# Moving six of 400 gathers from GpSimd to SyncE, one row at a time

## The chip, the cores and the metric

The kernel runs on one core of one Trainium2 chip. The metric is the device time of one execution in microseconds (us), the median of several runs. The core has five engines with a queue of instructions each: TensorE (PE: matrix products and transposes, weight loads shown apart as PEld), VectorE (DVE), ScalarE (ACT), GpSimd (POOL) and SyncE (SP), which here only issues DMAs. All DMAs of the core run on the same 16 DMA engines.

## The reference

The inputs are `seq` (1024 x 50 item numbers), `lengths` (1024), a table `emb` of 100001 rows of 128 floats, whose row 0 counts as zeros, and `gamma` and `beta`, 128 each.

```python
e = emb[seq]                                   # 1024 x 50 x 128
prefix = jnp.cumsum(e, axis=1)
denom = jnp.minimum(t_idx[None, :], lengths[:, None])
uF = prefix / denom[:, :, None]
mean, var = uF.mean(axis=0), uF.var(axis=0)    # over the 1024 sequences
y = (uF - mean) * lax.rsqrt(var + BN_EPS) * gamma + beta
def step(v, x):                                # 50 steps in time
    v = v + (x - v) / TAU
    spike = (v - V_TH >= 0)
    return v - spike * V_TH, spike
uF_out = spikes.mean(axis=0)                   # 1024 x 128
scores = uF_out @ emb.T                        # 1024 x 100001
```

## The kernel before

The work has two stages. In the **first**, the 50 time steps run one after the other. A step t needs 1024 rows of the table, one for each sequence. They are fetched by eight indirect DMAs of GpSimd (line 207, `gather(t)`), each of which brings 128 rows of 512 bytes into a 128 x 128 block of the tile `e_t`: partition p of block n holds the row of sequence 8p + n. Two tiles `e` alternate (`gp`, two buffers), and `gather(t + 2)` stands in the program behind the transposes of step t, since it writes the tile that these have read. For each block TensorE transposes the rows and adds them into the running sum in PSUM (line 324, tiles `pre`, two halves of 512 sequences). VectorE scales the sum (line 335), takes its statistics (336, 342), and with ScalarE makes the normalized input, the state `v` and the spike counts (298, 301, 353, 359 to 372, 376, 379, 294). The order in which the instructions stand on each engine is the order of the program text; nothing reorders them afterwards.

In the **second** stage the counts, 128 features by 1024 sequences, are the weights of matrix products with the transposed table (`product`, line 160), and the results go out as `scores`, 409.6 MB (line 169, from SyncE). The counts are in three tiles: `countA` for the first 128 sequences, `countB` for the next 512, `countC` for the last 384. They are written at the end of step 49 and read to the end of the kernel. The table is loaded for this stage in pieces of 1024 rows (`fetch`, line 109). The first loads, some 20 MB, stand at the front of SyncE's queue; at t = 44 one more follows there (line 405), and then the stores of `scores`.

DMAs that SyncE and ScalarE issue report to eight counters in turn (DMAHW0 to DMAHW7), and a DMA is issued only once the one before it on its counter has landed: at most eight are under way. GpSimd's DMAs do the same with DMASW0 to DMASW7.

Of the kernel before, what the change touches and what calls it, by code (L numbers as in the profile page):

```python
# [12 lines left out]
F32 = mybir.dt.float32  # L13
BF16 = mybir.dt.bfloat16
F32R = mybir.dt.float32r
I32 = mybir.dt.int32
U32 = mybir.dt.uint32
AF = mybir.ActivationFunctionType
ALU = mybir.AluOpType

P = 128
# [4 lines left out]
BANK = 512  # L26
# [4 lines left out]
ASIDE = 2  # L31
SHIFT = TWICE + ASIDE
FURTHER = {5: 1, 6: 2}

WIDTHS = 4 * [2] + 4 * [3] + 13 * [6]
NARROW, MIDDLE = 4, 8
# [3 lines left out]
def rec_kernel(  # L40
# [9 lines left out]
    nc = tc.nc  # L50
    B, T = seq.shape
    N, D = table.shape
    NB = B // P
# [6 lines left out]
    const = ctx.enter_context(tc.tile_pool(name="const", bufs=1))  # L60
# [6 lines left out]


    countA = const.tile([P, P], F32R, tag="countA", name="countA")
    countB = const.tile([P, BANK], F32R, tag="countB", name="countB")  # L70
    countC = const.tile([P, B - BANK - P], F32R, tag="countC", name="countC")
    counts = [countA]
    counts += [countB[:, k : k + P] for k in range(0, BANK, P)]
    counts += [countC[:, k : k + P] for k in range(0, B - BANK - P, P)]
    ident = const.tile([P, P], F32, tag="ident", name="ident")


# [94 lines left out]
    with ExitStack() as ph:  # L172
# [6 lines left out]
        vp = ph.enter_context(tc.tile_pool(name="v", bufs=1, space=bass.MemoryType.PSUM))  # L179

        idx = once.tile([P, NB, T], I32, tag="idx", name="idx")
# [21 lines left out]

        def gather(t):
            es[t] = gp.tile([P, B], F32, tag="e", name=f"e_{t}")
            for n in range(NB):
                nc.gpsimd.indirect_dma_start(  # L207
                    out=es[t][:, n * P : (n + 1) * P],
                    out_offset=None,
                    in_=table,  # L210
                    in_offset=bass.IndirectOffsetOnAxis(ap=idx[:, n, t : t + 1].bitcast(U32), axis=0),
                )

        make_identity(nc, ident)
        isz = up.tile([P, NB, P], F32, tag="uF", name="isz")
        rb = up.tile([P, NB, P], F32, tag="uF", name="rb")
        gather(0)

        nc.vector.memset(isz, 0.0)
        for u in (0, P // 2):  # L220
# [70 lines left out]
        def over(t, v):  # L291

            d = lp.tile([P, B], BF16, tag="d", name=f"d_{t}")
            nc.scalar.activation(d, v, AF.Identity, bias=less)  # L294
            return d

        def rest(d, v, cs):
            nc.vector.scalar_tensor_tensor(negv[:, cs], d[:, cs], 0.0, v[:, cs], ALU.is_ge, ALU.subtract)
# [18 lines left out]
        for t in range(T):  # L317
            last = t == T - 1
            e = es.pop(t)
            uF = up.tile([P, B], F32, tag="uF", name=f"uF_{t}")  # L320
            bs = sp.tile([P, B // BANK, 6], F32, tag="bs", name=f"bs_{t}")
            for h, cs in enumerate(halves):
                for k in range(0, BANK, P):
                    nc.tensor.matmul(  # L324
                        pre[h][:, k : k + P],
                        lhsT=e[:, h * BANK + k : h * BANK + k + P],
                        rhs=ident,
                        start=False,
                        stop=last,
                        is_transpose=True,  # L330
                        skip_group_check=True,
                    )
                    if last and h and k + P < BANK:
                        keep_busy(ident, KQ // 2)
                nc.vector.scalar_tensor_tensor(uF[:, cs], rlen[:, cs], 1.0 / (t + 1), pre[h], ALU.max, ALU.mult)  # L335
                nc.vector.bn_stats(bs[:, h, :], uF[:, cs])
            if t + 2 < T:
                gather(t + 2)
            if not last:
                correct(t + 1, l)  # L340
            mv = sp.tile([P, 2], F32, tag="mv", name=f"mv_{t}")
            nc.vector.bn_aggr(mv, bs.rearrange("p h s -> p (h s)"))  # L342


            r = sp.tile([P, 1], F32, tag="r", name=f"r_{t}")
            nc.scalar.activation(r, mv[:, 1:2], AF.Sqrt, bias=eps)  # L346
            if last:
# [12 lines left out]
            q = sp.tile([P, 1], F32, tag="q", name=f"q_{t}")  # L360
            a = sp.tile([P, 1], F32, tag="a", name=f"a_{t}")
            if last:
                nc.vector.tensor_scalar(q, w, r, r, ALU.mult, ALU.mult)
                nc.vector.scalar_tensor_tensor(q, q, 3.0, r, ALU.subtract, ALU.mult)
                vA = once.tile([P, P], F32, tag="r0n", name="vA")
                nc.vector.scalar_tensor_tensor(vA, centred, q, near, ALU.mult, ALU.add)
                nc.vector.scalar_tensor_tensor(countA, vA, -2.0 * V_TH, count[:, pieceA], ALU.is_le, ALU.add)
                nc.vector.tensor_mul(a, q, hgb[:, 0:1])
            else:
                nc.vector.scalar_tensor_tensor(q, mv[:, 1:2], BN_EPS, r, ALU.add, ALU.mult)  # L370
                nc.vector.tensor_scalar(q, q, r, 3.0, ALU.mult, ALU.subtract)
                nc.vector.tensor_scalar(a, q, r, hgb[:, 0:1], ALU.mult, ALU.mult)  # L372


            def x(vt, cs):
                nc.scalar.activation(vt, uF[:, cs], AF.Identity, bias=hgb[:, 1:2], scale=a)  # L376

            def step(vt, cs):
                nc.vector.scalar_tensor_tensor(vt, negv[:, cs], -0.5, vt, ALU.mult, ALU.add)  # L379

            if not last:
                vt = vp.tile([P, B], F32, tag=f"v{(t + 1) % 2}", name=f"v_{t}")
                x(vt, whole)
                if t:
                    spiked(count, whole, v)
                step(vt, whole)
                v = vt
                if t == T - 2:
                    spiked(count, whole, v)
                    moved = once.tile([P, P], F32, tag="r0hi", name="moved")  # L390
                    nc.vector.tensor_scalar_add(moved, v[:, pieceA], beta2)
                    near = once.tile([P, P], F32, tag="r0", name="near")
                    nc.vector.scalar_tensor_tensor(near, v[:, pieceA], V_TH, moved, ALU.is_ge, ALU.subtract)
                d = over(t, v)
                if t + 2 < T:
                    l = only(t + 2)

                if t in (T - 8, T - 6):
                    q = (t - T + 8) // 2
                    pair(q)  # L400
                    prepare(q, vp.tile([P, HALF], F32, tag="v0", name=f"pt_{q}"))
                    if q == TWICE - 1:
                        for k in range(TWICE):
                            rows[GROUP + ASIDE + k] = first[:, k, :]
                        nc.sync.dma_start(
                            out=first[:, :TWICE, :],
                            in_=table[(GROUP + ASIDE) * HALF : (GROUP + SHIFT) * HALF, :].rearrange(
                                "(q p k) d -> p q (k d)", p=P, k=KQ
                            ),
                        )  # L410

        keep_busy(near, 2 * KQ)
        for cs in (pieceB, pieceC):
            nc.scalar.activation(uF[:, cs], uF[:, cs], AF.Identity, bias=mv[:, 0:1], scale=-1.0)

# [45 lines left out]
    for c, W in enumerate(WIDTHS):  # L464
# [21 lines left out]
        def ready():  # L486
            nonlocal to_split, third
            if to_split < q2 + FURTHER.get(c, 0) and free:
                prepare(to_split, psum.tile([P, HALF], F32, tag="ps", name=f"pt_{to_split}"))
# [13 lines left out]
        for n, q in blockwise:  # L503
            if n not in os:
                pool, tag, most = turns[blocks % len(turns)]
                blocks += 1
                os[n] = pool.tile([P, most * HALF], F32, tag=tag, name=f"o_{c}_{n}")
            o = os[n]
# [27 lines left out]
            if n in (1, 4) and c >= MIDDLE and to_fetch < parts:  # L536
                g, k = divmod(to_fetch - SHIFT, GROUP)
# [26 lines left out]
```

## Time and profile before

| | us |
|---|---|
| median of three runs | 1571.3 (1571.26 to 1571.34) |
| profiled execution, its own span | 1570.1 |
| GpSimd busy, 400 gathers among 406 instructions | 381.0 |
| TensorE matmul busy | 1130.3 |
| VectorE busy | 948.4 |
| ScalarE busy | 674.3 |

The span of the profiled execution goes from its first to its last instruction; the median of the runs stands 1.2 us above it. A row of the timeline gives start, duration, engine, line, operation, written and read tile, how many were merged, and in brackets how long the engine was idle before it and what ended that. "SPq" and "ACTq" mark DMAs that SyncE and ScalarE issue; their duration is that of issuing, not of the transfer. A row of the waits gives the time in total, the number of times and the longest. A row of the windows gives the busy time of each engine in a stretch, then the granted TensorE clock, the share of the DMA engines' time and the GB/s moved.

### The profile page before, as it was taken

The page shows a single profiled execution, that of the slowest core. Times are in us where ns is not written, and L with a number is a line of the kernel's source. Part 1 is how long each engine was busy: PE and PEld are TensorE (multiplying, and loading weights), DVE is VectorE, ACT ScalarE, POOL GpSimd, SP SyncE. Part 2 cuts the span into 40 slices and gives each one's busy share as a digit, 9 for nine tenths or more (in the row PEclk, how much of TensorE's full clock was granted, in tenths as well). Part 3 has the DMA queues.
Part 4 walks back from the last instruction along what each step waited for, and adds up shares of the span by engine and source line. Part 5 has one row for each costly group of instructions (what it writes and reads, how often), then busy time and mean ns, then how long its engine had stood idle before and what let it go on. Part 6 is the DMA issues. An engine that isn't in the chain of part 4 may idle for free.

```text
span 1570.1 us, 12251 instructions
## 1 busy us (share of the span) xinstructions
PE 1130.3 (72%) x4464; PEld 803.4 (51%) x4464; DVE 948.4 (60%) x1126; ACT 674.3 (43%) x698; POOL 381.0 (24%) x406
## 2 busy tenths in 40 slices
PE   4544444444445998899878888887888878888884
PEld 2211111111122776667766666665666656666663
DVE  5777777767778656666555555555555545555552
ACT  2333333333333545555444444444444444444442
POOL 7777777777776000000000000000000000000000
PEclk9999999999995999999999899999999999899997
DMA  9711111111121999999999999999999999999998
GB/s 347 265 52 52 53 52 53 52 53 54 52 79 49 374 413 404 423 416 404 426 428 430 428 427 415 423 423 430 405 421 426 412 432 409 429 430 420 423 388 364
DMA packets 51457, 488.12 MB, mean 311 GB/s; under 512 B 10095, under 2 KB 10352, under 8 KB 30276
## 3 DMA queue, kind: packets, MB, share of 16 engines
q1 hardware_dynamic: 30896, 430.86, 65.3%
q0 software_dynamic: 12800, 26.24, 5.7%
q10 hardware_dynamic: 7700, 30.23, 4.7%
q8 instruction: 35, 0.57, 0.1%
q14 instruction: 26, 0.21, 0.0%
HBM read 77.69 MB, written 409.60 MB: 310 GB/s over the span
## 4 chain that ended last, share of the span: by engine, by line
DMA 51%; POOL 18%; PE 14%; issue 8%; DVE 5%; ACT 3%; POOLq 0%; ACTq 0%; SPq 0%; DVEq 0%
DMA scores<-o 44%; POOL e L207 18%; PE po L160 13%; DMA e<-in_L_rec_emb_table,idx 7%; DVE o L519 3%; ACT o L521 3%; DVE pairs L153 1%; ACT pairs L152 1%; PE pt L136 0%; PE pre L324 0%; ACT hi L152 0%; DVE lo L153 0%; DMA idx<-in_r_seq 0%; ACTq L521 0%; POOLq L560 0%
## 5 line engine op out<-in xcount | busy, mean ns | idle before, releaser
L519 DVE TENSOR_SCALAR o<-po 128x1024 f32<-128x1024 f32 (+1 forms) x390 | 466.4, 1214 | 324.6 <-DMA scores<-o 178.7
L521 ACT ACTIVATE o<-po 128x1024 f32<-128x1024 f32 x392 | 393.4, 1026 | 496.8 <-DMA scores<-o 352.6
L207 POOL DMA_INDIRECT e<-in_L_rec_emb_table,idx x400 | 380.3, 951 | 123.9 <-issue 110.4
L324 PE MATMUL pre<-ident,e 128*128 128x128 f32 x400 | 180.1, 463 | 227.1 <-DMA e<-in_L_rec_emb_table,idx 226.2
L160 PE MATMUL po<-pairs,countB 128*128 128x512 f32 (+1 forms) x1120 | 290.7, 406 | 58.0 <-ACT o L521 58.0
L160 PE MATMUL po<-pairs,countC 128*128 128x512 f32 (+1 forms) x840 | 241.2, 435 | 56.6 <-ACT o L521 48.4
L160 PEld LDWEIGHTS po<-pairs,countB 128*128 128x128 f32 x1120 | 210.9, 193 | 117.9 <-ACT o L521 75.6
L324 PEld LDWEIGHTS pre<-ident,e 128*128 128x128 f32 x400 | 73.5, 184 | 337.1 <-DMA e<-in_L_rec_emb_table,idx 336.2
L160 PEld LDWEIGHTS po<-pairs,countC 128*128 128x128 f32 x840 | 169.0, 209 | 108.4 <-ACT o L521 60.1
L153 DVE TENSOR_TENSOR pairs<-pt,pairs 128x1024 fp32r<-128x1024 f32 x70 | 85.2, 1218 | 96.6 <-ACT pairs L152 96.5
L335 DVE SCALAR_TENSOR_TENSOR uF<-rlen,pre 128x512 f32<-128x512 f32 x100 | 68.3, 683 | 110.3 <-PE pre L324 110.3
L136 PE MATMUL pt<-ident,rows 128*128 128x128 f32 (+1 forms) x768 | 105.9, 284 | 9.7 <-issue 4.9
L346 ACT ACTIVATE r<-mv,eps 128x1 f32<-128x1 f32 x50 | 14.8, 295 | 222.5 <-DVE mv L342 222.5
L136 PEld LDWEIGHTS pt<-ident,rows 128*128 128x128 f32 (+1 forms) x768 | 95.4, 148 | 27.1 <-issue 11.4
L160 PE MATMUL po<-hi,countB 128*128 128x512 f32 x208 | 86.0, 413 | 12.0 <-ACT o L521 11.7
L282 PE MATMUL pre<-zT,ls 128*128 128x512 f32 x100 | 78.1, 783 | 22.8 <-DVE uF L335 18.9
L152 ACT CAST pairs<-pt 128x1024 fp32r<-128x1024 f32 x70 | 70.1, 1013 | 42.2 <-PE pt L136 42.2
L160 PE MATMUL po<-lo,countB 128*128 128x512 f32 x208 | 83.4, 401 | 0.0
L294 ACT ACTIVATE d<-v,less 128x1024 bf16<-128x1024 f32 x49 | 54.6, 1114 | 65.4 <-DVE v L379 62.3
L160 PE MATMUL po<-hi,countC 128*128 128x512 f32 x156 | 67.0, 429 | 15.7 <-ACT o L521 14.0
L376 ACT ACTIVATE v<-uF,hgb,a 128x1024 f32<-128x1024 f32 x49 | 59.2, 1208 | 30.5 <-DVE a L372 30.5
L160 PE MATMUL po<-pairs,countA 128*128 128x512 f32 x280 | 69.1, 396 | 4.2 <-ACT o L521 4.1
(88 smaller groups left out, 856.0 us busy)
## 6 DMA issues: line engine op xcount, KB each, us to landing
scores<-o SPq DMA_DIRECT2D x96, 3072.0 KB, 19.7
scores<-o SPq DMA_DIRECT2D x32, 1536.0 KB, 8.9
scores<-o SPq DMA_DIRECT2D x29, 1024.0 KB, 7.1
rows<-in_L_rec_emb_table ACTq DMA_DIRECT2D x19, 1536.0 KB, 29.7
scores<-o SPq DMA_DIRECT2D x8, 2896.5 KB, 17.1
rows<-in_L_rec_emb_table SPq DMA_DIRECT2D x5, 3072.0 KB, 34.6
e<-in_L_rec_emb_table,idx POOLq DMA_INDIRECT x400, 2.5
rows<-in_L_rec_emb_table SPq DMA_DIRECT2D x2, 1024.0 KB, 5.4
```

The source lines that it names most:

```text
L136: nc.tensor.transpose(pt[:, k0 : k0 + pw], r[:pw, k0 : k0 + D], ident[:pw, :pw])
L152: nc.scalar.copy(vh, vp)
L153: nc.vector.tensor_tensor(vl, vp, vh.bitcast(F32), ALU.subtract)
L160: nc.tensor.matmul(po[:, :kw], lhsT=counts[n], rhs=part[:, k0 : k0 + kw], start=j == 0, stop=j == 1,)
L207: nc.gpsimd.indirect_dma_start(out=es[t][:, n * P : (n + 1) * P], out_offset=None, in_=table, in_offset=bass.IndirectOffsetOnAxis(ap=idx[: ...
L282: nc.tensor.matmul(pre[h], lhsT=l, rhs=zT[:, h * BANK : (h + 1) * BANK], start=t == 0, stop=False, skip_group_check=True,)
L294: nc.scalar.activation(d, v, AF.Identity, bias=less)
L324: nc.tensor.matmul(pre[h][:, k : k + P], lhsT=e[:, h * BANK + k : h * BANK + k + P], rhs=ident, start=False, stop=last, is_transpose=True, ...
L335: nc.vector.scalar_tensor_tensor(uF[:, cs], rlen[:, cs], 1.0 / (t + 1), pre[h], ALU.max, ALU.mult)
L376: nc.scalar.activation(vt, uF[:, cs], AF.Identity, bias=hgb[:, 1:2], scale=a)
L519: nc.vector.tensor_scalar_mul(o[:, h0 : h0 + hw], po[:, :hw], 1.0 / T)
L521: nc.scalar.mul(o[:, h0 : h0 + hw], po[:, :hw], 1.0 / T)
```

## The change

In the steps 12, 19, 26, 33, 40 and 47 GpSimd fetches seven blocks instead of eight. The 128 rows of the eighth block are fetched by SyncE. To begin with, VectorE copies the item numbers of block 7 as floats, TensorE turns them (steps on the partitions, sequences along the row), and VectorE multiplies them by 512 and writes them as integers: the byte address of each row. SyncE loads sixteen addresses at a time into sixteen registers (line 226 of the new text, TENSOR_LOAD) and issues sixteen DMAs of 512 bytes with the registers as source addresses (line 229), eight times for one block. The six blocks go to four places in turn in the memory of `countB` (`held_rows`); the addresses stand in that of `countC` (`ids`). Both counts are now allocated behind the last step. `fetch_singles(0)` stands before the steps, and `fetch_singles(i + 1)` at the step that uses block i; on SyncE nothing stands between them.

```diff
+BY_SYNC = (12, 19, 26, 33, 40, 47)
+AT_ONCE = 16
...
+    held_rows = const.tile([P, BANK], F32, tag="countB", name="held_rows")
+    ids = const.tile([P, B - BANK - P], F32, tag="countC", name="ids")
...
         def gather(t):
-            for n in range(NB):
+            for n in range(NB - (t in BY_SYNC)):
                 nc.gpsimd.indirect_dma_start(
...
+        byte_rows = table.rearrange("n d -> (n d)").bitcast(U8)
+        starts = ids[:T, :P].bitcast(I32)
+        regs = [nc.sync.alloc_register(f"row{k}") for k in range(AT_ONCE)]
+        def fetch_singles(i):
+            t = BY_SYNC[i]
+            rows_of = held_rows[:, i % (BANK // P) * P :][:, :P]
+            singles[t] = rows_of
+            for p0 in range(0, P, AT_ONCE):
+                nc.sync.load(regs, starts[t : t + 1, p0 : p0 + AT_ONCE])
+                for k, reg in enumerate(regs):
+                    at = nc.sync.snap(reg, donate=True, min_val=0, max_val=(N - 1) * row_bytes)
+                    nc.sync.dma_start(
+                        out=rows_of[p0 + k : p0 + k + 1, :].bitcast(U8),
+                        in_=byte_rows[bass.ds(at, row_bytes)].rearrange("(o b) -> o b", o=1),
+                    )
...
         gather(0)
+        last_ids = ids[:, P : P + T]
+        nc.vector.tensor_copy(last_ids, idx[:, NB - 1, :])
+        ips = vp.tile([P, B], F32, tag="v0", name="ips")
+        nc.tensor.transpose(ips[:T, :P], last_ids, ident)
+        nc.vector.tensor_scalar_mul(starts, ips[:T, :P], float(row_bytes))
+        fetch_singles(0)
...
-                        lhsT=e[:, h * BANK + k : h * BANK + k + P],
+                        lhsT=singles[t] if h * BANK + k + P == B and t in singles else e[...],
...
                 gather(t + 2)
+            if t in BY_SYNC[:-1]:
+                fetch_singles(BY_SYNC.index(t) + 1)
```

On SyncE, at the end of the first loads of the table, this stood before (the name behind DMA is the written tile, then the read one; in brackets what it waits for). The load of line 405 follows directly:

```order
L109 DMA rows_112<-in_L_rec_emb_table 128x6x1024 [waits DMAHW2_49]
L109 DMA rows_114<-in_L_rec_emb_table 128x6x1024 [waits DMAHW3_49]
L109 DMA rows_116<-in_L_rec_emb_table 128x6x1024 [waits DMAHW4_49]
L405 DMA rows_103<-in_L_rec_emb_table 128x2x1024 [waits DMAHW5_49,DVE_49,PE_49]
L169 DMA scores<-o_0_2398 128x512 [waits DMAHW6_49,Activation_49]
```

And this stands there now (`held_rows` is the place of the single rows):

```order
L110 DMA rows_114<-in_L_rec_emb_table 128x6x1024 [waits DMAHW3_49]
L110 DMA rows_116<-in_L_rec_emb_table 128x6x1024 [waits DMAHW4_49]
L226 TENSOR_LOAD ids [waits DVE_49]
L229 DMA held_rows<-in_L_rec_emb_table 1x512 [waits DMAHW5_49]
L229 DMA held_rows<-in_L_rec_emb_table 1x512 [waits DMAHW6_49]
L229 DMA held_rows<-in_L_rec_emb_table 1x512 [waits DMAHW7_49]
L229 DMA held_rows<-in_L_rec_emb_table 1x512 [waits DMAHW0_49]
L229 DMA held_rows<-in_L_rec_emb_table 1x512 [waits DMAHW1_49]
L229 DMA held_rows<-in_L_rec_emb_table 1x512 [waits DMAHW2_49]
L229 DMA held_rows<-in_L_rec_emb_table 1x512 [waits DMAHW3_49]
L229 DMA held_rows<-in_L_rec_emb_table 1x512 [waits DMAHW4_49]
```

768 single rows and 48 register loads now stand between the last of the first loads and the load of line 405. The eighth single row uses the same counter, DMAHW4, as the last large load.

On TensorE, the end of step 12 (`e_641` is the tile of that step, `pre_182` the second half of the sum) before:

```order
L324 MATMUL pre_182<-ident,e_641 128x128 [waits DMASW4_49]
L324 MATMUL pre_182<-ident,e_641 128x128 [waits DMASW5_49]
L324 MATMUL pre_182<-ident,e_641 128x128 [waits DMASW6_49]
L324 MATMUL pre_182<-ident,e_641 128x128 [waits DMASW7_49]
L282 MATMUL pre_181<-zT,ls 128x512 [waits DVE_49]
```

And now (`e_781` is the tile of step 12):

```order
L351 MATMUL pre_322<-ident,e_781 128x128 [waits DMASW4_49]
L351 MATMUL pre_322<-ident,e_781 128x128 [waits DMASW5_49]
L351 MATMUL pre_322<-ident,e_781 128x128 [waits DMASW6_49]
L351 MATMUL pre_322<-ident,held_rows 128x128 [waits DMAHW4_49,DMAHW5_49,DMAHW3_49,DMAHW6_49,DMAHW2_49,DMAHW7_49,DMAHW1_49,DMAHW0_49]
L309 MATMUL pre_321<-zT,ls 128x512 [waits DVE_49]
```

The last of the eight transposes of the step waits for SyncE's counters in place of GpSimd's.

More of the change, by code (lines that the diff above doesn't have):

```diff
@@ L17 @@
 U32 = mybir.dt.uint32
+U8 = mybir.dt.uint8
 AF = mybir.ActivationFunctionType
@@ L69, in rec_kernel @@
     countA = const.tile([P, P], F32R, tag="countA", name="countA")
[L70 to L74, printed above, removed]
+    held_rows = const.tile([P, BANK], F32, tag="countB", name="held_rows")
+    ids = const.tile([P, B - BANK - P], F32, tag="countC", name="ids")
     ident = const.tile([P, P], F32, tag="ident", name="ident")
@@ L212, in gather @@
                 )
+        byte_rows = table.rearrange("n d -> (n d)").bitcast(U8)
+        row_bytes = 4 * D
+        starts = ids[:T, :P].bitcast(I32)
+        regs = [nc.sync.alloc_register(f"row{k}") for k in range(AT_ONCE)]
+        singles = {}
+        def fetch_singles(i):
[10 more added lines that the diff above has]
+                    )
         make_identity(nc, ident)
@@ L325, in rec_kernel @@
                         pre[h][:, k : k + P],
-                        lhsT=e[:, h * BANK + k : h * BANK + k + P],
+                        lhsT=singles[t] if h * BANK + k + P == B and t in singles else e[:, h * BANK + k : h * BANK + k + P],
                         rhs=ident,
@@ L410, in rec_kernel @@
                         )
+        countB = const.tile([P, BANK], F32R, tag="countB", name="countB")
+        countC = const.tile([P, B - BANK - P], F32R, tag="countC", name="countC")
+        counts = [countA]
+        counts += [countB[:, k : k + P] for k in range(0, BANK, P)]
+        counts += [countC[:, k : k + P] for k in range(0, B - BANK - P, P)]
         keep_busy(near, 2 * KQ)
```

## The prediction

> **What bounds the kernel now.** I read the page's busy shares, then its chain of waits, then the windows of the two stages.
>
> ```profile
> PE 1130.3 (72%) x4464; PEld 803.4 (51%) x4464; DVE 948.4 (60%) x1126; ACT 674.3 (43%) x698; POOL 381.0 (24%) x406
> DMA 51%; POOL 18%; PE 14%; issue 8%; DVE 5%; ACT 3%; POOLq 0%; ACTq 0%; SPq 0%; DVEq 0%
> ```
> ```profile
> core 0: us, PE busy (x) PEld busy (x) DVE busy (x) ACT busy (x) POOL busy (x), PEclk, DMA share, GB/s
> 80.00:512.00 432.00, 207.61 (x475) 89.57 (x476) 313.87 (x538) 160.15 (x177) 321.87 (x341) 0.96 0.19 54
> 512.00:1570.00 1058.00, 885.89 (x3901) 696.28 (x3900) 582.73 (x493) 487.22 (x492) 0.00 (x0) 0.94 0.99 416
> ```
>
> The shares mislead: POOL is the idlest engine over the span, yet it is busy 321.9 of 432 us in the first stage and never in the second, where the DMA engines are full (0.99) with the output. The stages touch once: a microsecond saved on the way to the last step starts the stores a microsecond earlier, and the second stage, limited by its bytes, moves with them.
>
> In the first stage, the waits and POOL's timeline:
>
> ```profile
> PE pre L324 <- DMA e<-in_L_rec_emb_table,idx: 226.2, 314, 2.5
> POOL e L207 <- issue: 110.4, 362, 0.3
> 85.38 0.95 POOL L207 DMA_INDIRECT e<-in_L_rec_emb_table,idx  x1 [0.30 <-issue]
> 86.63 0.94 POOL L207 DMA_INDIRECT e<-in_L_rec_emb_table,idx  x1 [0.30 <-issue]
> 504.57 0.94 POOL L207 DMA_INDIRECT e<-in_L_rec_emb_table,idx  x1 [0.30 <-issue]
> 512.89 6.65 SPq L169 DMA_DIRECT2D scores<-o  x8
> ```
>
> TensorE waits for gathered rows 314 times; POOL waits for nothing but its own issue (0.30 us each time, 362 times). One gather takes 86.63 - 85.38 = 1.25 us, the last starts at 504.57, and the first stores go out 8.3 us behind it. POOL's issue rate bounds the stage.
>
> **What the change takes away.** Six gathers at 1.25 us: 7.5 us. The tail behind the last gather and the second stage stay as they are, so this is the gain if SyncE's rows are there when their transposes come.
>
> **When the rows are needed.** Eight transposes make a step, so step 12 ends with the 104th and step 47 with the 384th. A count of line 324 up to 135.5 gives 103 of them, up to 486 gives 383:
>
> ```profile
> L324 PE MATMUL pre<-ident,e x103: 415/474/477, 16.4 to 135.4; 128*128 128x128 f32 x103
> L324 PE MATMUL pre<-ident,e x383: 327/474/478, 16.4 to 485.8; 128*128 128x128 f32 x192
> 135.39 0.48 PE L324 MATMUL pre<-ident,e 128*128 128x128 f32 x1 [0.80 <-DMA e<-in_L_rec_emb_table,idx]
> 485.78 0.47 PE L324 MATMUL pre<-ident,e 128*128 128x128 f32 x1 [0.74 <-DMA e<-in_L_rec_emb_table,idx]
> 487.67 0.69 DVE L335 SCALAR_TENSOR_TENSOR uF<-rlen,pre 128x512 f32<-128x512 f32 x1 [2.60 <-PE pre L324]
> 497.59 0.69 DVE L335 SCALAR_TENSOR_TENSOR uF<-rlen,pre 128x512 f32<-128x512 f32 x1 [2.47 <-PE pre L324]
> ```
>
> With seven gathers the eighth transpose can follow the seventh: block 0 is due at 135.4 + 0.5 = 135.9, and block 5, after five saved gathers, at 485.8 + 0.5 - 6.25 = 480.0. Lateness there is partly caught up: VectorE, the next busiest in a step, idles 2.60 and 2.47 us in the two steps after 47, so 5.1 us late costs nothing at the end, and GpSimd goes on meanwhile, since the tile that it overwrites isn't the one waited for.
>
> **When SyncE can deliver.** Its timeline at the start, three windows, and the few rows that resemble a single-row fetch:
>
> ```profile
> 0.75 0.39 SPq L182 DMA_DIRECT2D idx<-in_r_seq  x1
> 1.19 0.42 SPq L184 DMA_DIRECT2D len_i<-in_r_lengths  x1
> 1.66 0.42 SPq L186 DMA_DIRECT2D r<-in_L_rec_emb_table  x1
> 2.13 0.43 SPq L188 DMA_DIRECT2D gb<-in_L_rec_gamma  x1
> 2.60 0.43 SPq L189 DMA_DIRECT2D gb<-in_L_rec_beta  x1
> 3.07 0.43 SPq L109 DMA_DIRECT2D rows<-in_L_rec_emb_table  x1
> 4.06 34.77 SPq L109 DMA_DIRECT2D rows<-in_L_rec_emb_table  x6
> 464.05 0.37 SPq L405 DMA_DIRECT2D rows<-in_L_rec_emb_table  x1
> ```
> ```profile
> 58.00:62.00 4.00, 2.38 (x5) 0.99 (x5) 2.11 (x5) 0.42 (x2) 3.09 (x4) 1.00 1.04 393
> 62.00:66.00 4.00, 2.19 (x6) 1.09 (x6) 3.69 (x8) 2.12 (x2) 3.08 (x4) 1.00 0.63 224
> 66.00:70.00 4.00, 2.52 (x6) 0.99 (x5) 3.90 (x8) 2.20 (x3) 3.08 (x4) 1.00 0.19 52
> ```
> ```profile
> 1407.74 0.38 ACTq L109 DMA_DIRECT2D rows<-in_L_rec_emb_table  x1
> 1449.41 0.49 ACTq L120 DMA_DIRECT2D rows<-in_L_rec_emb_table  x1
> 1449.93 0.82 ACTq L125 DMA_DIRECT2D rows<-in_L_rec_emb_table  x1
> gb<-in_L_rec_beta SPq DMA_DIRECT2D x1, 0.5 KB, 2.3
> ```
>
> SyncE has issued the large loads by 4.06 + 34.77 = 38.8, but the eighth single row shares its counter with the last of them. The DMA share falls from 1.04 to 0.19 between 62 and 66: the loads have landed by about 65, and there the stream really begins. From then it is 761 rows (eighth to last) and 47 register loads. With c for a row's issue and l for a register load of sixteen, the last row lands at 65 + 761c + 47l + 2.3 (the landing of a half-kilobyte DMA, last row above), and the first block at 65 + 121c + 7l + 2.3.
>
> *c.* The nearest rows are SyncE's own small loads at the start, issued back to back as the new ones are: (3.07 - 0.75) / 5 = 0.465; I take 0.47. Low end 0.37 (line 405, alone). High end 0.52, from ScalarE's line 120 to its line 125 (1449.93 - 1449.41): line 120 is one row of 512 bytes, the very shape, but on another engine. An address from a register is on no row; it can only add. Eight rows under way at 0.47 give each 3.8 us to land, more than 2.3, so the counters don't hold the stream.
>
> *l.* No row shows it. It can't be below nothing, and hardly above 2.3, the whole trip of a small DMA with its completion. [...]
>
> So block 0 lands at 65 + 56.9 + 7 + 2.3 = 131.2, 4.7 early, and block 5 at 65 + 357.7 + 47 + 2.3 = 472.0, 8.0 early; those between lie between. The waits cost nothing, by a small margin.
>
> **The rest.** The six transposes that wait for eight counters stand where TensorE idles 0.74 to 0.80 us anyway. At the start VectorE and TensorE get three small instructions ahead of line 221; the rows
>
> ```profile
> 16.40 2.12 PE L324 MATMUL pre<-ident,e 128*128 128x128 f32 x8
> 25.14 0.94 POOL L207 DMA_INDIRECT e<-in_L_rec_emb_table,idx  x1 [0.30 <-PE pre L324]
> ```
>
> show the first tile read by 18.5 and overwritten from 25.1, so a microsecond there is covered; without the 6.6 us of cover it would be paid in full. Line 405's load and the first stores now queue behind SyncE's stream, which ends its issue at 469.7: the load slips some 13 us from 464.05 - 6.25 and is used only in the second stage; the stores (512.9 before) aren't reached. From block 4 on SyncE also waits for the transpose of step 12 or 19, long past. The bytes moved are the same.
>
> Sum against the profiled execution: 1570.1 - 7.5 = 1562.6. The median of the runs lies 1.2 us above that execution: **1563.8 us**.
>
> **Rival 1, slower: SyncE's price for a row is that of line 120.** Line 120 costs 0.49 where the same engine's large load costs 0.38, so one row alone is dearer by 0.11; added to SyncE's 0.37 and the 0.04 between its issues that makes 0.52 too. Then the last block lands at 65 + 396.5 + 47 + 2.3 = 510.8, 30.8 late; less 5.1 caught up and 7.5 gained, +18.2: 1589.5 us. It decides from c = (480 + 5.1 + 7.5 - 114.3) / 761 = 0.497 on. Against it: one row, on another engine; for it: the shape, and that register addresses are still unpaid. [...]
>
> **Rival 2, slower: the register loads.** At l = 2.3 and c = 0.47 the end is 533.1, net +40.5: 1612 us. It decides from l = 1.44. Nothing in the trace speaks either way. [...]
>
> **Rival 3: nothing gained.** The rows come at the break-even of rival 1, or the second stage starts earlier and doesn't end earlier: 1571. Against the latter: DMA share 0.99.
>
> **How the numbers follow.** In time, 1563.8 (1562 to 1566): 0.50, since SyncE's own rate and the middle of l both fit, but with 8 us to spare of 405. Rival 1: 0.27, up to some 60 us if registers cost more. Rival 2: 0.17, of which the page's rule 0.05. Rival 3: 0.06. What a measurement of this kernel tells from no change is about 0.2%, 3 us. Range 1561.5 to 1612: from the gain with a little noise to rival 2's bound; above stay the dearest of both rivals, some 0.15. Faster 0.50, same 0.06, slower 0.44.
>
> **What would show it.** Right: line 229 issued every 0.47 us or less, TENSOR_LOAD near 1 us, held_rows transposes with no idle time of their own, the last gather near 497, first stores near 505. Wrong: TensorE waits on the DMA held_rows that grow from block to block and are longest at step 47, with SyncE busy without a gap from 65 on; or first stores at 505 and an end that hasn't moved.

## The result and the profile after

The change takes 1564.07 us (1563.98 to 1564.39) where before takes 1571.32 on the same chip: 7.25 us less, ratio 0.9954 with an interval of 0.9940 to 0.9968. The forecast was 1563.8.

The twelve runs of the study went to five chips: on three of them before takes 1571.3 us as in the first run, on two it takes 1636 to 1638 with the same code, so each run below stands only beside before on its own chip, and I call these chips "the first kind" and "the second kind".

The page after, its busy shares and its chain of waits, then the windows of the two stages:

```profile
PE 1118.9 (72%) x4465; PEld 794.4 (51%) x4465; DVE 948.1 (61%) x1128; ACT 673.4 (43%) x698; POOL 374.5 (24%) x400
DMA 47%; POOL 19%; PE 13%; issue 10%; DVE 5%; ACT 4%; ACTq 0%; POOLq 0%; SPq 0%; DVEq 0%
```
```profile
core 0: us, PE busy (x) PEld busy (x) DVE busy (x) ACT busy (x) POOL busy (x), PEclk, DMA share, GB/s
80.00:505.00 425.00, 207.79 (x479) 90.80 (x479) 314.69 (x537) 160.93 (x178) 315.66 (x334) 1.00 0.22 56
505.00:1562.00 1057.00, 875.15 (x3896) 685.78 (x3896) 580.76 (x492) 485.45 (x491) 0.00 (x0) 0.95 0.99 417
```

POOL is still in the chain, SyncE's queue (SPq) at 0%: GpSimd still sets the end of the first stage. Up to the first stores that stage is 8.2 us shorter; from there to the end of the span the second takes 1057.7 us, before 1057.2. The timeline gives the two ends (the last gather stood at 504.57, the first stores at 512.89), and the rows of line 351, the new transposes, say whether anyone waited for SyncE:

```profile
496.29 0.94 POOL L208 DMA_INDIRECT e<-in_L_rec_emb_table,idx  x1 [0.30 <-issue]
504.70 14.95 SPq L170 DMA_DIRECT2D scores<-o  x12
L351 PE MATMUL pre<-ident,held_rows x6: 444/446/448, 135.3 to 479.2; 128*128 128x128 f32 x6
  DMA held_rows<-in_L_rec_emb_table: 0.4, 2
```

The last gather comes 8.28 us earlier, the first stores 8.19. The six transposes stand between 135.3 and 479.2, where the working had put them (135.9 and 480.0), and TensorE waited 0.4 us for the rows in all. So the forecast came out. But it came out with another margin than it named. SyncE's instructions by line (least, median and most ns of one; first and last start), and its waits:

```profile
L229 SPq MOVE held_rows<-in_L_rec_emb_table x768: 29/29/29, 40.5 to 380.8; - x192
L229 SPq DMA_DIRECT2D held_rows<-in_L_rec_emb_table x768: 227/228/7166, 40.6 to 380.8; - x192
L226 SPq TENSOR_LOAD <-ids x48: 1200/1256/1426, 39.3 to 374.6; - x48
SPq L229 <- DMA rows<-in_L_rec_emb_table: 14.8, 2, 8.7
375.95 5.12 SPq L229 DMA_DIRECT2D held_rows<-in_L_rec_emb_table  x16
457.10 0.41 SPq L434 DMA_DIRECT2D rows<-in_L_rec_emb_table  x1
```

A row is one DMA of 0.228 us and one register MOVE of 0.029; sixteen take 5.12, so c = 5.12 / 16 = 0.32, not 0.47. A load of sixteen takes l = 1.256, not 1.0. The stream was issued by 380.8, with the last block not due before 479: almost a hundred microseconds of margin, not eight.

### The profile page after: what moved, and what is told of

Read it like the earlier page. It is cut to its first block, busy times and chain, and to the rows that moved or that the text cites. A ratio compares the mean times of both kernels' runs of the same rounds, so it can differ in the third digit from the quotient of the medians.

```text
span 1562.4 us, 13860 instructions
## 1 busy us (share of the span) xinstructions
PE 1118.9 (72%) x4465; PEld 794.4 (51%) x4465; DVE 948.1 (61%) x1128; ACT 673.4 (43%) x698; POOL 374.5 (24%) x400
## 4 chain that ended last, share of the span: by engine, by line
DMA 47%; POOL 19%; PE 13%; issue 10%; DVE 5%; ACT 4%; ACTq 0%; POOLq 0%; SPq 0%; DVEq 0%
DMA scores<-o 45%; POOL e L208 19%; PE po L161 13%; DVE o L553 3%; ACT o L555 3%; DMA e<-in_L_rec_emb_table,idx 3%; DVE pairs L154 1%; ACT pairs L153 0%; PE pt L137 0%; PE pre L351 0%; ACT hi L153 0%; PE warm L337 0%; DMA idx<-in_r_seq 0%; DVE lo L154 0%; ACTq L555 0%
## 5 line engine op out<-in xcount | busy, mean ns | idle before, releaser
L208 POOL DMA_INDIRECT e<-in_L_rec_emb_table,idx x394 | 373.8, 949 | 122.1 <-issue 117.1
L351 PE MATMUL pre<-ident,e 128*128 128x128 f32 x394 | 174.9, 463 | 220.7 <-DMA e<-in_L_rec_emb_table,idx 220.1
L161 PE MATMUL po<-pairs,countC 128*128 128x512 f32 (+1 forms) x840 | 230.9, 421 | 57.5 <-ACT o L555 49.0
L161 PEld LDWEIGHTS po<-pairs,countC 128*128 128x128 f32 x840 | 162.2, 200 | 107.0 <-ACT o L555 60.7
L375 ACT ACTIVATE r<-mv,eps 128x1 f32<-128x1 f32 x50 | 14.8, 295 | 212.2 <-DVE mv L371 212.2
```

What stands on the lines that cost most here:

```text
L161: nc.tensor.matmul(po[:, :kw], lhsT=counts[n], rhs=part[:, k0 : k0 + kw], start=j == 0, stop=j == 1,)
L208: nc.gpsimd.indirect_dma_start(out=es[t][:, n * P : (n + 1) * P], out_offset=None, in_=table, in_offset=bass.IndirectOffsetOnAxis(ap=idx[: ...
L351: nc.tensor.matmul(pre[h][:, k : k + P], lhsT=singles[t] if h * BANK + k + P == B and t in singles else e[:, h * BANK + k : h * BANK + k + P],
```

## Experiments

Two theories stood against each other. **A**: GpSimd's 1.25 us per gather is the price, six times over, and SyncE's stream is free while its rows are in time; where they are late, the lateness of the last block sets the end. **B**: the stream itself takes something (gathers, instruction supply, DMA engines), and what was gained is less than what the gathers cost.

### The gathers without the stream, and the stream without the gathers

Seven gathers in the six steps, the eighth transpose reading zeros, no addresses and no stream:

```diff
-            fetch_singles(...)
+        nc.vector.memset(held_rows, 0.0)
```

> GpSimd gathers seven blocks in the six steps; nothing fetches the eighth, and TensorE reads a tile of zeros there, so the 768 rows are left out of the sums. Theory A: as fast as the changed kernel, 1563.8 us (1571.3 - 7.5), within 0.5. Rival B: faster than the changed kernel by what the stream costs, 1 us or more. Rival C: near 1571.

Measured, on a chip of the second kind: 1630.9 beside 1637.55, ratio 0.9956 (0.9938 to 0.9974), 6.65 us less. The change had 0.9954 on the first kind, so six gathers fewer are enough for its gain. The two ratios come from different kinds of chip, though, and on the second kind GpSimd's rate is not the only limit. Its row from 100 to 220 us, and two rows of the waits:

```profile
L207 POOL DMA_INDIRECT e<-in_L_rec_emb_table,idx x84 | 79.9, 951 | 42.0 <-issue 25.4 <-remote 10.6 <-PE pre L285 5.4
DVE uF L338 <- remote: 126.1, 22, 10.7
POOL e L207 <- remote: 48.8, 11, 5.5
```

"remote" is idle time that ended with a signal whose sender the profile does not show. The stream alone, four and one address to a load and the change show such waits on the second kind too, 57 to 156 us of them on VectorE and 22 to 59 on GpSimd; on the first kind before, the change and the stream alone show none. So 84 blocks are gathered here in 120 us, without any stream, where before gathers 97 on the first kind.

All 400 gathers and the change's stream into memory that nobody reads:

```diff
-            for n in range(NB - (t in BY_SYNC)):
+            for n in range(NB):
...
-                        lhsT=singles[t] if h * BANK + k + P == B and t in singles else e[...],
+                        lhsT=e[...],
```

> SyncE's 768 single rows are fetched as in the changed kernel, but GpSimd gathers all eight blocks of every step and TensorE reads those; the single rows are read by nobody. Theory A (the gain is six gathers of GpSimd's issue rate, and the stream on SyncE is free): the kernel takes as long as before, 1571.3 us, within 0.5. Rival B (the stream itself disturbs the gathers or the DMA engines, and the change gains less than it saves): over 1572. Rival C (something else in the change, such as the new places of the counts, brings the gain): near 1564.

> All 400 gathers stay on GpSimd, and SyncE runs the change's stream of 768 rows into memory that nobody reads, again, for a chip on which before takes 1571 us. Theory A (the stream is free as long as it ends before the first stores, at 381 us of 513): 1571.3, ratio 1.000 (0.999 to 1.001), GpSimd's gathers every 1.25 us while it runs. Theory B (SyncE's rows and instruction fetches take from the gathers): the last gather later than before's 504.6 by as much as the kernel is slower, 1 us or more. In the study of two blocks 1.55 us of 2.5 came back, in the change 7.25 of 7.5: by B the stream would cost 1 us per 128 us, 3 us here, 1574. On a chip like the second, as before: 1790 beside 1638.

On a chip of the first kind (the second text) it took 1572.22 beside 1571.31, ratio 1.0006 (0.9997 to 1.0016). GpSimd's rows of the stretch in which the stream runs, of this kernel; the stream's last issue; and the two ends:

```profile
L208 POOL DMA_INDIRECT e<-in_L_rec_emb_table,idx x97 | 91.5, 944 | 29.6 <-issue 29.0 <-DMA e<-in_L_rec_emb_table,idx 0.6
L229 SPq DMA_DIRECT2D held_rows<-in_L_rec_emb_table x768: 227/228/7015, 40.9 to 380.8; - x192
503.49 0.94 POOL L208 DMA_INDIRECT e<-in_L_rec_emb_table,idx  x1 [0.30 <-issue]
511.92 7.61 SPq L170 DMA_DIRECT2D scores<-o  x8
```

97 gathers in the 120 us from 100 on are one per 1.24 us, with the stream beside them, and last gather and first stores come no later than before's. A holds: the stream takes nothing from the first stage. This kernel and the change differ only in the six gathers and in which rows six transposes read, and they take 1572.22 and 1564.07 us on chips with the same time before. So nothing else in the change brings the gain, and rival C falls. The 0.9 us are not explained: within the interval they are nothing, but every run of this kernel lies above every run of before, and in the profile they would have to lie behind the first stores (1570.2 - 511.92 = 1058.3, before 1570.1 - 512.89 = 1057.2).

On a chip of the second kind (the first text) the same kernel took 1789.55 beside 1637.55, ratio 1.0913 (1.0884 to 1.0942). By its number that is theory B. But the stream takes nothing from the gathers here either: 86 blocks in 120 us (100 to 220 and 440 to 560) beside the stream, 84 and 85 without it. The time is lost where the stream ends, behind the last gather (568.3):

```profile
730.88 0.41 SPq L434 DMA_DIRECT2D rows<-in_L_rec_emb_table  x1
731.38 13.34 SPq L170 DMA_DIRECT2D scores<-o  x10
```

The first stores stand behind the stream in SyncE's queue. `countB`, which lies in the memory of `held_rows`, can't be written before the stream has ended either: VectorE waited 144.2 us for that. Both waits end together, so this run doesn't tell what either would cost alone.

### More register loads

Four addresses, then one, to a load instead of sixteen, for the price of l and for late rows:

```diff
-AT_ONCE = 16
+AT_ONCE = 4     # e3; 1 in e4
```

> The changed kernel with four addresses to a register load instead of sixteen: 192 loads instead of 48. In the changed kernel a load of sixteen took 1.26 us, and a row without a load 0.323 us. If a load costs 0.079 us for each register (or 0.31 for each 16 bytes), four cost about 0.31, a row takes on average about the same 0.41, the stream ends near 390 and the kernel stays at 1564. If most of 1.26 is a fixed price, say 0.9, four cost 1.0: a row takes 0.58 on average, the last block lands near 65 + 761 x 0.58 + 2 = 508, 28 us behind its step, and by the prediction's law (less 5.1 caught up and 7.5 gained) the kernel takes 1571.3 + 15.4 = 1587.

> The changed kernel with a register load for each row: 768 loads. If a load costs 0.079 us for each register alone, a row takes 0.323 + 0.08 + 0.06 = 0.46, the stream ends near 420 and the kernel stays at 1564. If the price is 0.31 for each 16 bytes begun, a row takes 0.69, the last block lands near 65 + 761 x 0.69 + 2 = 592, 112 us late, and by the prediction's law the kernel takes 1571.3 + 112 - 5.1 - 7.5 = 1671. With a fixed price of 0.9 a load, a row takes 1.28, the last block lands near 1041, and the kernel takes about 2120. Whatever the price, the law says: the end moves by the lateness of the last block less 12.6 us. If GpSimd is held up as well (the claim is that it isn't), the end is later than that.

1833.58 and 2109.35, one run each, beside 1637.55 on a chip of the second kind. The numbers expected were worked out from the first chip's prices and don't apply to these times; the law that the second text states is taken up with the nine blocks below. As prices of a load, the medians do tell something:

```profile
L226 SPq TENSOR_LOAD <-ids x192: 2/562/733, 38.7 to 747.9; - x192
L226 SPq TENSOR_LOAD <-ids x768: 2/493/1404, 39.8 to 1023.5; - x192
```

One register 0.49, four 0.56, sixteen 1.26 (1.24 on this kind of chip, in the run of the next section). Up to four a load is nearly all fixed price; from four to sixteen each register adds 58 ns, and at sixteen that makes 79 ns a register.

### The change itself on the second kind

> The changed kernel itself, unaltered, timed and profiled beside the kernel before on the same chip. In the first run SyncE issued a row every 0.323 us and a block of 128 rows took 53 us, so that block 5's rows had been fetched some 98 us ahead of its step. Theory A (GpSimd's 1.25 us per gather bounds the first stage, SyncE has time to spare): ratio to before 0.995, 7 us less, last issue of the stream near 381 us. Theory B (SyncE's time for an instruction is not a constant: it was 0.7 us and more in the study of the stream alone, where before itself took 1637 us): where SyncE's rows come every 0.7 us or slower, the stream ends past 700 us, the first stores wait behind it, and the kernel is 100 to 200 us slower than before on that chip.

1782.38 (1777.99 to 1784.98) beside 1636.35, ratio 1.0893 (1.0866 to 1.0920): 9% slower. The two runs above add up to almost that: the stream costs 152.0, the gathers give 6.65, together +145.4, against a measured +146.0 on another chip of that kind. That they agree so well is luck, since the stream ends at 730.5 there and at 693 here, and the first stores wait for different things. Why the stream takes so long shows in the stream alone. Its line 229 in 440 to 560 us, where GpSimd gathers, and in 570 to 690, behind the last gather (568.3), both 120 us long; between them GpSimd's row of the first stretch:

```profile
L229 SPq DMA_DIRECT2D held_rows<-in_L_rec_emb_table x94: 3/228/1407, 440.7 to 558.8; - x94
L208 POOL DMA_INDIRECT e<-in_L_rec_emb_table,idx x86 | 81.4, 947 | 39.2 <-issue 24.4 <-remote 14.2 <-DMA e<-in_L_rec_emb_table,idx 0.6
L229 SPq DMA_DIRECT2D held_rows<-in_L_rec_emb_table x286: 19/228/705, 569.3 to 689.9; - x143
```

94 rows beside 86 gathers; 286 rows without a gather, the rate of the first chip (289 in 120 us, there with 97 gathers beside them). So on the second kind, and only there, SyncE is slow while GpSimd gathers. The median of a DMA issue stays 228 ns, but it hides two other groups: of 347 issues between 100 and 560 us 129 take 0.65 to 0.75 us and 105 less than 0.02 us, and the mean is 0.36 us (0.23 behind the last gather). The register MOVE does the same: its mean is 0.30 us there and 0.029 behind the last gather. In the change, in a bad stretch from 200 to 265 us, and what follows from it:

```profile
L229 SPq MOVE held_rows<-in_L_rec_emb_table x43: 3/690/1384, 200.9 to 264.2; - x43
PE pre L351 <- DMA held_rows<-in_L_rec_emb_table: 238.8, 6, 47.3
693.51 0.41 SPq L434 DMA_DIRECT2D rows<-in_L_rec_emb_table  x1
718.09 25.16 SPq L170 DMA_DIRECT2D scores<-o  x16
```

690 ns in this stretch instead of 29; over the whole run the median of the MOVE is 29 here too. TensorE waits 239 us for the six blocks, the stream ends at 693, and the first stores go out at 718, where they went out at 569 in the run without a stream. The text's theory B has the size right, but not the path: the stores go out 24.6 us behind the end of the stream, so they did not wait for the queue, but for the steps from 47 on, which waited for the last block. That instructions reach SyncE late is a reading that fits both, but it is not shown. Between 80 and 500 us the packets that load instructions took a median of 0.50 us in the stream alone and 0.43 in the same kernel on the first kind, and a packet brings many instructions (the stream's 1584 take 12 more packets of 8 KB: 38 in the change, 26 in before, both on the first kind), while in the stream alone about four in ten of SyncE's instructions between 100 and 560 us take 0.65 us or more. What ties the slow instructions to the gathers on these chips, and whether the "remote" waits have the same cause, stays open.

### More blocks

Eight and nine gathers instead of six, to find the edge:

```diff
-BY_SYNC = (12, 19, 26, 33, 40, 47)
+BY_SYNC = (11, 16, 21, 27, 32, 37, 43, 48)          # e5, e12
+BY_SYNC = (11, 16, 21, 26, 31, 35, 39, 43, 47)      # e6, e11
```

> Eight gathers instead of six leave GpSimd, at steps 11, 16, 21, 27, 32, 37, 43 and 48, about as close as SyncE's stream of 53 us per block allows. Theory A: two more gathers are 2.5 us more, so about 1561.6 us where the change took 1564.1, ratio to before 0.9938; by the measured stream the blocks land at 117, 170, 223, 277, 330, 383, 436 and 489 us and are due at 125, 174, 222, 281, 330, 378, 437 and 485, so up to 5 us late, which costs at most 3 us of it if it is not caught up: 1561.6 to 1565. Theory B (SyncE's time for an instruction is not the same everywhere): where a block takes 100 us, the last lands near 870 and the kernel is 300 us or more above before.

> Nine gathers leave GpSimd, at steps 11, 16, 21, 26, 31, 35, 39, 43 and 47, more than SyncE's stream can supply in time. By the law of the prediction (the stage ends when the last block has come, less 5.1 us caught up) with the measured 53.2 us per block, block 8 lands at 114.8 + 8 x 53.2 + 2.3 = 542.7 us; it is due at 486.3 - 8 x 1.25 = 476.3; 66.4 late, less 5.1, less 9 x 1.25 saved: 50 us above before, 1621 us (1611 to 1631), last gather near 550, TensorE waiting on the DMA held_rows in waits that grow from block to block. Rival (late rows are absorbed, since GpSimd and VectorE have idle time to catch up with): below 1575 us.

Both fell on a chip of the second kind: 1858.84 and 1913.58 beside 1636.35 (ratios 1.1350, 1.1325 to 1.1374, and 1.1689, 1.1653 to 1.1725), since the stream ended at 793 and 829 us. For the eight, theory B had 300 us or more above before; it is 222. Neither number of the texts for the first kind could be tried, and the edge stayed open. Then on the first kind:

> Nine gathers leave GpSimd, at steps 11, 16, 21, 26, 31, 35, 39, 43 and 47; of the earlier run the chip was one on which before took 1636 us, so the law of the prediction was not put to its own numbers. On a chip like the first (before 1571 us), where SyncE takes 53.2 us per block. Theory A (the first stage ends when the last block has come, less 5.1 us that VectorE catches up): block 8 lands at 114.8 + 8 x 53.2 + 2.3 = 542.7 us, due at 486.3 - 8 x 1.25 = 476.3, so 66.4 late, less 5.1, less 9 x 1.25 saved: 50 us above before, 1621 us (1611 to 1631); last issue of the stream at 540, first stores not before it; TensorE's waits on the DMA held_rows begin with the blocks at steps 31 to 35 and add up to 60 to 70 us. Theory B (late rows hold GpSimd up as well, so that each late block costs its lateness anew and none of the saved gathers comes back): above 1640. Rival (late rows are caught up in idle time): below 1575. On a chip like the second, as before: 1914 us beside 1636.

1626.19 beside 1571.27, ratio 1.0350 (1.0333 to 1.0368): 54.9 above before, where the law of the prediction gave 50. The chain of this kernel, the transposes of the last two blocks, TensorE's waits for rows (us and times), one gather behind a late block, and SyncE's last rows; below them, from before, the last transpose of step 47:

```profile
DMA 45%; SPq 25%; PE 13%; issue 7%; DVE 5%; ACT 4%; ACTq 0%; DVEq 0%
489.48 0.45 PE L351 MATMUL pre<-ident,held_rows 128*128 128x128 f32 x1 [21.05 <-DMA held_rows<-in_L_rec_emb_table]
542.92 0.45 PE L351 MATMUL pre<-ident,held_rows 128*128 128x128 f32 x1 [23.82 <-DMA held_rows<-in_L_rec_emb_table]
  DMA held_rows<-in_L_rec_emb_table: 111.5, 7
493.48 0.94 POOL L208 DMA_INDIRECT e<-in_L_rec_emb_table,idx  x1 [15.09 <-PE pre L351]
541.62 0.41 SPq L434 DMA_DIRECT2D rows<-in_L_rec_emb_table  x1
565.32 3.14 SPq L170 DMA_DIRECT2D scores<-o  x5
```
```profile
487.15 0.48 PE L324 MATMUL pre<-ident,e 128*128 128x128 f32 x1 [0.90 <-DMA e<-in_L_rec_emb_table,idx]
```

POOL has gone from the chain, and SPq has its place. The last block's transpose was due at 486.3 - 8 x 1.25 = 476.3 and came at 542.92, 66.6 late; the first stores follow it by 22.4 us, where before they follow the same transpose by 512.89 - 487.15 = 25.7. So 3.3 us were caught up, not 5.1, and the law holds: the end moves with the lateness of the last block, and no block's lateness is paid anew. The waits are another matter. The text had 60 to 70 us of them, and there are 111.5: each late block holds TensorE anew, and GpSimd too (15.09 us here), and some 45 us of it are made up between the late blocks.

The law holds on the second kind as well, over a wide range of lateness. From the load of line 434, which follows the last row on SyncE, to the first stores there are 23.7 us here, and 23.8, 24.2, 24.6 and 24.6 in the runs with four and with one address to a load, with the change and with nine blocks on the second kind, in which that load stands at 750, 1025, 694 and 829 us.

> Eight gathers leave GpSimd, at steps 11, 16, 21, 27, 32, 37, 43 and 48, again, for a chip on which SyncE takes 53.2 us per block. Theory A (GpSimd's 1.25 us per gather bounds the stage while the rows are in time): blocks land at 117, 170, 223, 277, 330, 383, 437 and 490 us and are due at 125, 174, 222, 281, 330, 378, 437 and 485; eight gathers are 10 us; the last block's lateness of 5 us is caught up but for 2 (in the study of nine blocks 3 us came back), so 8 to 10 us less than before: 1561 to 1563, ratio 0.9936 to 0.9950, at or below the change's 1564.1. Theory B (each late block costs anew): blocks 2, 4, 5 and 7 are each a few us late, together 11, and nothing is gained, 1568 or more. On a chip like the second, as before: 1859 beside 1636.

1561.52 (1561.19 to 1565.02) beside 1571.31, ratio 0.9937 (0.9923 to 0.9951): 9.8 us less, the fastest version. Its waits for rows, in us and times, the end of its stream, its last gather and the first stores:

```profile
  DMA held_rows<-in_L_rec_emb_table: 7.3, 4
488.02 0.41 SPq L434 DMA_DIRECT2D rows<-in_L_rec_emb_table  x1
494.01 0.94 POOL L208 DMA_INDIRECT e<-in_L_rec_emb_table,idx  x1 [0.30 <-issue]
504.82 10.09 SPq L170 DMA_DIRECT2D scores<-o  x9
```

TensorE waits four times for rows, 7.3 us together, and nearly the whole 10 us arrives in the median all the same. The profiled execution is the slowest of the five, with 1565.02. In it the last gather comes 10.6 us earlier than before, but the first stores only 8.1: the tail between them is 10.8 us instead of 8.3, which is what a last block late by 5 us and caught up by some 3 would leave. Why the other four executions end 3 to 4 us sooner is not shown, since none of them has a trace.

### Fewer blocks

```diff
-BY_SYNC = (12, 19, 26, 33, 40, 47)
+BY_SYNC = (22, 39)
```

> Two gathers instead of six leave GpSimd, at steps 22 and 39. In the study of the stream alone on a chip on which before took 1637 us, SyncE issued 7 to 16 instructions per 10 us while GpSimd gathered and 44 to 55 once the gathers had ended (blocks 3 to 5 took 53.2 us each, blocks 0 to 2 between 165 and 185), and the steps of TensorE were about 11.3 us long. Theory A (the change fails there only because rows come late and the first stores queue behind the stream): with two blocks, ready near 225 and 404 us and due near 260 and 450, no step waits on the DMA held_rows, the stream ends before the first stores by 150 us, and two gathers are saved: 2.5 us less than before, ratio 0.9985 (0.996 to 1.000); last gather about 2 us earlier than before's. Theory B (SyncE's instructions and GpSimd's gathers take from each other, so that each block of rows costs the gathers time): the stream slows gathers and TensorE while it runs, some 4 us or more for its 400 us, ratio 1.001 to 1.01. On a chip like the first one (before 1571 us), both: 2.5 us less, 1568.8.

It fell on a chip of the first kind: 1569.70 beside 1571.25, ratio 0.9991 (0.9982 to 1.0000), 1.55 less of 2.5 expected. The interval holds the 2.5 (0.9984) as well as nearly nothing; it is too near the limit of the measurement to decide anything. In its trace the last gather (501.01) and the first stores (509.45) come 3.6 and 3.4 us earlier than before, so the first stage gives the 2.5 in full; from the first stores to the end, though, it takes 1058.6 us, where before takes 1057.2. The stream alone showed the like (1058.3), and that too stays open. What it was made for, the second kind, it did not see.

### What one issue costs, by shape

```diff
+    nc.sync.dma_start(out=o, in_=r)     # 128 times each: 1, 128 x 4 B, 16, 2 rows
...
+    nc.scalar.dma_start(out=ids[j : j + 1, 2 * P :], in_=table[j : j + 1, :])     # 3 in each of steps 20 to 27
```

> Prices of a DMA issue on SyncE by shape, with fixed addresses and no register: block 2 has 128 DMAs of one row of 512 bytes, block 3 has 128 of 128 partitions by 4 bytes, block 4 has 128 of 16 partitions by 512 bytes, block 5 has 128 of 2 partitions by 512 bytes; ScalarE issues 3 single rows in each of steps 20 to 27. It fetches fixed rows instead of the wanted ones for four of the six blocks. The prediction's price of 0.47 us came from rows of 128 partitions, the change measured 0.228 us and an interval of 0.323. Theory A (the number of descriptors sets the price): one row 0.23, two about the same, 16 partitions between, 128 partitions 0.33 to 0.47 us each. Theory B (the engine's ring was what made the start dear, not the shape): all four shapes 0.23 us. And by the prediction's rival, single rows on ScalarE cost 0.49 us, or, if line 120's price has to do with what stood around it, 0.23.

It ran once, on a chip of the second kind (1707.39 beside 1636.35), so only the medians count; the issues of 0.7 us and more are that chip's. Line 235 in the stretches of the four shapes (one row; 128 partitions; sixteen; two), and line 438, ScalarE's single rows:

```profile
L235 SPq DMA_DIRECT2D held_rows<-in_L_rec_emb_table x124: 2/251/797, 288.3 to 372.7; - x124
L235 SPq DMA_DIRECT2D held_rows<-in_L_rec_emb_table x127: 2/430/724, 373.9 to 453.7; - x127
L235 SPq DMA_DIRECT2D held_rows<-in_L_rec_emb_table x126: 3/418/1386, 456.5 to 545.0; - x126
L235 SPq DMA_DIRECT2D held_rows<-in_L_rec_emb_table x126: 3/252/713, 546.4 to 606.4; - x126
L438 ACTq DMA_DIRECT2D ids<-in_L_rec_emb_table x24: 223/244/507, 303.7 to 390.1; - x24
```

One or two rows cost 0.25 us, sixteen or 128 partitions 0.42 to 0.43: the shape makes the price (A), except that sixteen is not between but already dear. ScalarE's single row costs 0.24, half of line 120's 0.49.

## Why the prediction was right, and where it was not

- **The gain, 7.5 us.** Right: 7.25 in the medians, 7.7 in the spans, 6.65 with the gathers taken away alone (second kind), 8.15 against the stream alone (first kind). The tail from last gather to first stores is 8.4 (8.3 before), the second stage as long as before to within a microsecond.
- **When rows are needed, 135.9 and 480.0.** Right, 135.3 and 479.2.
- **The stream begins at 65.** Right: SyncE waited 14.8 us for the large loads, and the eighth row and those behind it follow.
- **c = 0.47.** The term that was mis-sized, by almost half: 0.32. The price was read from rows of the right engine and the wrong shape: SyncE's small loads at the start write 128 partitions. The run on shapes gives these 0.43 and a single row 0.25, from issue to issue 0.474 and 0.295. With an address from a register it is 0.228 + 0.029 for its MOVE and 0.323 from row to row, so the address added some 0.03. Even the low end of the range, 0.37, was too high.
- **l = 1.0.** No run shows this term: a load of sixteen took 1.256, within the bounds of nothing and 2.3. With both measured, the prediction's own sum gives 65 + 761 x 0.323 + 47 x 1.32 + 2.3 = 375 (1.32: from row to row over a load 1.64, less 0.323), with the measured 380.8 it is 383. The 8 us between them are rows slower than the median: the 713 intervals without a load average 0.333. The form of the sum was right; its main price was not.
- **"A small margin", and the chance of 0.44 for slower.** On the first kind wrong: 96 us early, far from the break-even. The edge is between eight and nine blocks. On the second kind the slower side came true, with waits for rows and SyncE busy to the end. There a row with its share of the loads took (693 - 65) / 761 = 0.83 us, above the sum's break-even of 0.497 + 47 x 1.0 / 761 = 0.56 (with the first kind's times of need). So the sum's condition is the right one there too, but not for a reason that the text names: single instructions are held up for 0.65 us and more, while the medians stay (0.228 for the issue, 1.24 for the load). The prediction knew of one kind of chip alone; that it was tried on that kind is luck as far as its text goes.
- **Rival 1.** Fell with line 120: a single row on ScalarE costs 0.24. What makes line 120 dear is not its shape. On SyncE a single row is, beside two, the cheapest of the four shapes (0.251 and 0.252; 0.418 for sixteen, 0.430 for 128 partitions).
- **Rival 2.** Fell: 1.256, not 2.3. The rule behind 0.05 of its 0.17 is shown by no run; the measured 1.256 is 79 ns a register for sixteen, and one register alone takes 0.49.
- **5.1 us caught up, GpSimd going on.** Not called on by the change. The nine blocks gave 3.3, and GpSimd did not go on: it waited up to 15 us for transposes behind a late block, which cost nothing only because the last block set the end.
- **The load behind the stream slips 13 us.** Wrong: it went out at 457.10, where 464.05 - 6.25 = 457.8 had been its time, since the stream had ended at 381.

So the answer was right for its main reason, GpSimd's rate, and its doubt was sized on the wrong row.

## What to carry to other kernels

When one engine's issue rate bounds a stage, taking n of its instructions away saves n times what one takes, as long as the substitute ends in time (here 6 x 1.25 = 7.5 us, of which 7.25 came); the test is the last need against the last delivery (here 479.2 against a last issue at 380.8), and if that is late, the end moves with its lateness, here less some 3 us and what the gathers gave (with nine blocks the last came 66.6 us late and the first stores 52.4). Price an added DMA from a row of the same shape: by how many partitions it writes before by which engine issues it (here 0.25 us for one row on SyncE and 0.24 on ScalarE, 0.43 for 128 partitions on SyncE). And a queue that was idle can hide stores behind it: where its instructions come slower than planned, both the rows and whatever stands behind them are late (here 146 us for the change on the second kind), so leave room for the slowest chip, not for the one measured.

## What was not expected of the hardware

- Chips differ: with the same code the change has a ratio of 0.995 on the first kind and 1.089 on the second, where SyncE's stream gets through 94 rows in 120 us beside the gathers and 286 without them. On the first kind it gets through 289 beside them.
- On the second kind, in the stream alone, about four in ten of SyncE's instructions, register MOVEs too, take 0.65 us and more while GpSimd gathers (100 to 560 us). Without a stream VectorE and GpSimd stand still there too, 126 and 49 us in that run, for a signal whose sender the profile doesn't show.
- An issue on SyncE costs 0.25 us for one or two rows and 0.42 to 0.43 for sixteen or 128 partitions.
- A register load costs 0.49 us for one, 0.56 for four (both on the second kind) and 1.26 for sixteen values.
